# Mixture-of-experts stage of a graph-attention kernel: the router's VectorE order written out, its list built before its experts and biases, and two row groups of the second half loaded and measured early

## Chip, cores and metric

The kernel runs on 1 core of one Trainium2 chip. The metric is the device time of one execution in microseconds (us); the time before is 2988.52 us, the median of 3 runs (2987.83 to 2989.67).

## What is computed

Two layers over x with 4096 rows of 256 columns. Each layer is a dense graph attention over a 4096 x 4096 adjacency matrix, then a feed-forward part; layer 0 has a 30-step recurrence, layer 1 a mixture of six experts of which every row uses two. The change lies wholly in this last part:

```
x = x + _L1_gnn_ref(L1_gnn_t, _layernorm(x, axis=-1), adj, ...)
x = x + _L1_ffn_ref((_layernorm(x, axis=-1))[None], ...)[0]

def _L1_ffn_ref(features, ...):
    rh = relu(features @ router_w1 + router_b1)
    expert_logits = softmax(rh @ router_w2 + router_b2)
    top_w, top_i = top_k(expert_logits, 2)
    routing_weights = softmax(top_w)
    h1 = relu(features x expert_w1 + expert_b1)      # per expert
    h2 = relu(h1 x expert_w2 + expert_b2)
    expert_out = h2 x expert_w3 + expert_b3
    return sum over the two chosen experts of routing_weight * expert_out
```

## The kernel before

**Stages.** Attention of layer 0, the recurrence, two attention passes of layer 1 and the mixture follow each other. Rows are worked in tiles of 128 and in groups of four tiles (512 rows, 512 KB). The mixture splits the eight groups into two halves: groups 0 to 3 (half 0) and 4 to 7 (half 1).

**The router, `route(h, ...)`.** It is a generator: each `yield` marks a step. Its loop over groups `g` measures a group (`over_std`: four `bn_stats` L101, four `bn_aggr` L103, plus an epsilon L105 on VectorE, then a power L106 on GpSimd), one turn later normalises it (`nmr` L1109, four pieces of `n` L1112), stores it to the DRAM tile `nd` (L1115, SyncE's queue), transposes it on TensorE (`tp` L1120), copies it out on ScalarE (`fT` L1121) and writes the row minus one into the sums' tile `acc` (L1122, ScalarE). Another turn later it multiplies by the router's first matrix (`ps_r` L1099), takes the relu (`rh` L1101, ScalarE), multiplies by the second (`ps_l` L1129) and adds the bias on VectorE (`lg` L1132). After the loop comes a chain of small VectorE operations on all rows of the half: softmax, the best two (L1142 to L1162), a running count per expert (L1164 to L1176, four matmuls in between), each row's place in a list sorted by expert (L1179 to L1213). Two one-hot matrices per choice (`ohh` L1219 and L1222, `ohl` L1224) and 32 matmuls (L1229) turn places into the list: for every tile of 128 places the rows to fetch (`source` L1257) and where results go (`dest` L1258). `seen`, `ex` and `expert` (L1238 to L1246) give each tile's expert, `ohe`, `sel` and `bsel` (L1261 to L1271) its biases, `ws` (L1274 to L1279) the routing weights.

**The experts.** There are 37 tiles per half, 74 in all. For tile i, `gather` (L1313) fetches 128 rows of `nd` by `source` with an indirect DMA of GpSimd; `turn` transposes them (`pt` L1324) and copies them on VectorE (`xT` L1326); `fetch` reads the tile's expert into registers (L1333) and copies that expert's first two matrices (`w` L1344, VectorE and ScalarE); `hidden` makes the two hidden layers (`ph` L1352, relu L1363 on ScalarE and L1365 on VectorE); `result` the output (`po` L1373, `ye` L1375) and scatters it (L1376, GpSimd). `combine` adds the weighted results to `acc` (L1402) and writes the output. Half 1's `route` is stepped once per expert tile, so it runs beside half 0's experts.

**What sets the order.** Instructions are put on the engines' queues in an order that a planner works out before the run: among those that it holds ready, the one that stands first in the program. Each engine and SyncE's DMA queue then keep to that order. Inside `tc.manual_schedule(engines=...)` the named engines' instructions keep the program's order among themselves; instructions from outside such a block can still be put between them. In the mixture before only four small matmuls stand in such a block. The attention's end (`u`, `e`, L473 to L627) is outside one as well.

**Data.** Attention loads groups 0 to 3 of `x3d` ahead into the four places of `ring`. Half 1's groups are loaded by `load` through `load_ahead` (L93) into the same places. The tiles of the pool `m_one` take the SBUF that attention's tiles had, in the order in which they are asked for. The experts' 18 weight loads (L1297, 256 KB each) and `b3` (L1298) are written in the program after the first four steps of `route(0)`.

Of the kernel before, what the change touches and what calls it, by code (L numbers as in the profile page):

```python
# [11 lines left out]
F32 = mybir.dt.float32  # L12
# [6 lines left out]
OP = mybir.AluOpType  # L19
# [4 lines left out]
P = 128  # L24
# [22 lines left out]
def gnn_ffn_kernel(ctx: ExitStack, tc: tile.TileContext, a: dict, out: bass.AP):  # L47
# [48 lines left out]
    def over_std(pool, src):  # L96

        st = pool.tile([P, G, 6], F32, name="ln_st")
        mv = pool.tile([P, G, 2], F32, name="ln_mv")
        for r in range(G):  # L100
            nc.vector.bn_stats(st[:, r, :], src[:, r, :])  # L101
        for r in range(G):
            nc.vector.bn_aggr(mv[:, r, :], st[:, r, :])  # L103
        rstd = pool.tile([P, G], F32, name="ln_rstd")
        nc.vector.tensor_scalar(rstd, mv[:, :, 1], EPS, None, op0=OP.add)  # L105
        nc.gpsimd.tensor_tensor(rstd, rstd, mhalf, OP.pow)  # L106
        return rstd, mv
# [877 lines left out]
    def runs_of(t, g):  # L985

        return t[g * GR : (g + 1) * GR, :].rearrange("(p r) c -> p r c", r=G)
# [31 lines left out]
    with ExitStack() as scope:  # L1019
# [1 line left out]
        T = 2 * NH // P + E - 1  # L1021
        one = scope.enter_context(tc.tile_pool(name="m_one", bufs=1))
        bT = one.tile([P, NB], F32, name="bT")
        acc = one.tile([P, NT, C], F32, name="acc")
        ws = one.tile([P, 2, NT], F32, name="ws")
        bsel = [one.tile([P, T, 2 * KC], F32, name=f"bsel{h}") for h in range(2)]
        expert = [one.tile([P, T], I32, name=f"expert{h}") for h in range(2)]
        dest = [one.tile([P, T], I32, name=f"dest{h}") for h in range(2)]
        source = [one.tile([P, T], I32, name=f"source{h}") for h in range(2)]
        ew = [one.tile([P, E, KC, C], F32, name=f"ew{i}") for i in range(3)]  # L1030
        b3 = one.tile([P, E, C], F32, name="b3")
        nd = [dram.tile([NH, C], F32, name=f"nd{h}") for h in range(2)]
        yd = [dram.tile([2 * NH + T * P, C], F32, name=f"yd{h}") for h in range(2)]
# [41 lines left out]
        def over(t, n=NTH, m=E):  # L1075
            return t[:, :, None].to_broadcast([P, n, m])

        def route(h, turned, bank):

            lg = rone.tile([P, NTH, E], F32, name="lg")  # L1080
            rows, stds, fTs, rhs = {}, {}, {}, {}

            def load(g):
                if h * NGH + g not in ahead:
                    load_ahead(x3d, h * NGH + g, runs_of)
                rows[g] = ahead.pop(h * NGH + g)

            load(0)
            load(1)
            for g in range(NGH + 2):  # L1090
                if g + 2 < NGH:
                    load(g + 2)
                if g < NGH:
                    stds[g] = over_std(rwork, rows[g])
                if 2 <= g:
                    ps = bank("ps_r")
# [6 lines left out]
                if 1 <= g <= NGH:  # L1103
                    u = g - 1
                    at = (h * NGH + u) * G
                    t = rows.pop(u)
                    rstd, mv = stds.pop(u)
                    nmr = rwork.tile([P, G], F32, name="nmr")
                    nc.vector.scalar_tensor_tensor(nmr, mv[:, :, 0], -1.0, rstd, op0=OP.mult, op1=OP.mult)  # L1109
                    n = rwork.tile([P, G, C], F32, name="n")  # L1110
                    for r in range(G):
                        nc.vector.tensor_scalar(  # L1112
                            n[:, r, :], t[:, r, :], rstd[:, r : r + 1], nmr[:, r : r + 1], op0=OP.mult, op1=OP.add
                        )
# [102 lines left out]
            for i in range(2):  # L1217
# [20 lines left out]
            nc.vector.tensor_tensor(  # L1238
                seen,
                along[:, :T, None].to_broadcast([P, T, E - 1]),  # L1240
                first[:, None, 1:].to_broadcast([P, T, E - 1]),
                OP.is_ge,
            )
# [13 lines left out]
            nc.vector.tensor_scalar(source[h], sf, float(NH - 1), None, op0=OP.min)  # L1257
            nc.vector.tensor_copy(dest[h], df)  # L1258
            yield
            ohe = rone.tile([P, T, E], F32, name="ohe")  # L1260
            nc.vector.tensor_tensor(  # L1261
                ohe, over(ex, T), along[:, None, :E].to_broadcast([P, T, E]), OP.is_equal
# [18 lines left out]
        with tc.tile_pool(name="r_ps", bufs=1, space=PSUM) as psum, tc.tile_pool(  # L1281
# [187 lines left out]
```

## Time and profile before

| what | value |
|---|---|
| median of 3 runs | 2988.52 us |
| the profiled execution's own time | 2978.01 us |
| its span, first to last instruction | 2976.1 us |
| mean granted TensorE clock | 0.979 |
| PE / DVE / ACT / POOL busy share of the span | 94% / 92% / 83% / 39% |
| last matmul of attention ends | about 2652.6 us from the span's start |
| first expert matmul starts | 2710.47 us |

PE is TensorE's matmuls and PEld its weight loads, DVE VectorE, ACT ScalarE, POOL GpSimd, SP SyncE with its DMA queue; L101 is line 101 of the kernel. The profiled execution is a different one from the timed runs and 10.5 us below their median. Times inside the profile count from the start of its span. A line of a timeline gives the start, the duration (of a run of like instructions, from the first start to the last end), engine, line, operation, what is written and read, and in brackets how long the engine was idle before and what ended it. A line of a table by stage gives for each engine the busy us and the number of instructions, then the granted TensorE clock, the DMA share and GB/s.

### The profile page before, as it was taken

The page shows a single profiled execution, that of the slowest core. Times are in us where ns is not written, and L with a number is a line of the kernel's source. Part 1 is how long each engine was busy: PE and PEld are TensorE (multiplying, and loading weights), DVE is VectorE, ACT ScalarE, POOL GpSimd, SP SyncE. Part 2 cuts the span into 40 slices and gives each one's busy share as a digit, 9 for nine tenths or more (in the row PEclk, how much of TensorE's full clock was granted, in tenths as well). Part 3 has the DMA queues.
Part 4 walks back from the last instruction along what each step waited for, and adds up shares of the span by engine and source line. Part 5 has one row for each costly group of instructions (what it writes and reads, how often), then busy time and mean ns, then how long its engine had stood idle before and what let it go on. Part 6 is the DMA issues. An engine that isn't in the chain of part 4 may idle for free. (4 is left out here: it accounts for less than half of the span.)

```text
span 2976.1 us, 82659 instructions
## 1 busy us (share of the span) xinstructions
PE 2800.0 (94%) x33923; PEld 2562.3 (86%) x33923; DVE 2740.5 (92%) x5769; ACT 2465.1 (83%) x3125; POOL 1157.6 (39%) x1084
## 2 busy tenths in 40 slices
PE   7899999979999999999998999999889999986996
PEld 5899999968888888888887999999789999975995
DVE  7999999999999999999998899999889999986775
ACT  6799999988888888888877999999789999963342
POOL 3000000079999999999982000000200000014663
PEclk9999999989999999999999999999999999997998
DMA  9998885053333333333353031121302132124253
GB/s 292 272 255 243 227 239 154 24 128 68 68 68 68 68 69 68 68 67 70 68 111 119 22 102 57 64 80 34 108 23 91 55 104 88 44 78 147 81 173 135
DMA packets 484451, 320.07 MB, mean 108 GB/s; under 512 B 416590, under 2 KB 445419, under 8 KB 477931
## 3 DMA queue, kind: packets, MB, share of 16 engines
q1 hardware_dynamic: 474034, 290.27, 36.3%
q0 software_dynamic: 7104, 19.41, 2.1%
q8 instruction: 268, 4.39, 0.6%
q10 hardware_dynamic: 2936, 5.11, 0.5%
q14 instruction: 109, 0.88, 0.1%
HBM read 183.00 MB, written 52.04 MB: 79 GB/s over the span
## 5 line engine op out<-in xcount | busy, mean ns | idle before, releaser
L520 PE MATMUL acc<-vals,st 128*128 128x130 f16 x12288 | 1433.2, 218 | 38.3 <-DVE u L473 29.9
L520 PE MATMUL acc<-vals,below 128*128 128x130 f16 x12288 | 1432.9, 221 | 12.8 <-DVE below L574 12.0
L462 ACT ACTIVATE st<-f1b,nf 128x1024 int8<-128x1024 f32 x1265 | 1334.8, 1143 | 33.4 <-PE acc L520 24.1
L520 PEld LDWEIGHTS <-below 128*128 128x128 fp8e4 x12288 | 1176.5, 96 | 52.9 <-issue 46.5
L520 PEld LDWEIGHTS <-st 128*128 128x128 fp8e4 x12288 | 1208.2, 98 | 9.4 <-DVE st L568 7.5
L936 PE MATMUL po<-wT,zT 128*128 128x256 f32 x1920 | 576.1, 382 | 5.8 <-DVE y L876 3.2
L939 PE MATMUL po<-w,zT 128*128 128x256 f16 x3840 | 578.0, 273 | 0.7 <-DMA zT<-z 0.7
L907 POOL TENSOR_TENSOR th<-th,y 128x1024 f32<-128x1024 f32 x232 | 549.1, 2367 | 14.9 <-DVE z_st L916 0.4
L939 PEld LDWEIGHTS <-zT 128*128 128x128 f16 x3840 | 376.7, 98 | 162.0 <-DMA zT<-z 1.4
L574 DVE TENSOR_TENSOR below<-m,st 128x1024 int32<-128x1024 int32 x384 | 470.0, 1224 | 32.6 <-DVE st L568 0.9
L568 DVE TENSOR_TENSOR st<-st,m 128x1024 int32<-128x1024 int32 x384 | 467.3, 1217 | 0.2
L876 DVE SCALAR_TENSOR_TENSOR y<-po,z_rs,bias 128x256 f32<-128x256 f32 x928 | 384.4, 477 | 1.8 <-PE tp L868 0.7
L916 DVE BATCH_NORM_STATS2 z_st<-z 128x6 f32<-128x256 f32 x960 | 335.8, 413 | 0.0
L936 PEld LDWEIGHTS po<-wT,zT 128*128 128x128 f32 x1920 | 291.1, 192 | 15.3 <-ACT zT L923 3.6
L892 ACT ACTIVATE z<-th 128x1024 f32<-128x1024 f32 x240 | 251.7, 1049 | 17.5 <-POOL th L907 16.7
L927 POOL TENSOR_TENSOR z_rs<-z_rs,mhalf 128x4 f32<-128x4 f32 x240 | 244.6, 1019 | 3.1 <-ACT z_rs L926 3.1
L906 ACT ACTIVATE th<-y 128x1024 f32<-128x1024 f32 x232 | 241.7, 1042 | 0.0
L923 ACT COPY zT<-tp 128x512 f32<-128x512 f32 x240 | 140.4, 585 | 90.8 <-PE tp L868 89.7
L460 DVE TENSOR_SCALAR st<-f1b,nf 128x1024 int8<-128x1024 f32 x271 | 201.2, 743 | 7.6 <-PE acc L520 7.6
L759 POOL TENSOR_TENSOR x_rs<-x_rs,mhalf 128x4 f32<-128x4 f32 x8 | 9.4, 1174 | 503.6 <-ACT x_rs L758 503.6
L1044 POOL IOTA along_i<- 128x512 int32 (+1 forms) x5 | 2.8, 556 | 486.7 <-PE acc L520 486.6
L437 POOL MEMSET hs<- 128x4 f32 x3 | 0.3, 99 | 492.8 <-DVE u L490 492.8
(263 smaller groups left out, 3158.8 us busy)
## 6 DMA issues: line engine op xcount, KB each, us to landing
ring<-in_adj_dram SPq DMA_DIRECT2D x64, 1024.0 KB
m<-edges SPq DMA_DIRECT2D x32, 1024.0 KB
f1b<-fd SPq DMA_DIRECT2D x48, 512.0 KB
edges<-m SPq DMA_DIRECT2D x16, 1024.0 KB
y<-yd SPq DMA_DIRECT2D x16, 512.0 KB
ew<-in_L_ffn_expert_w_dram SPq DMA_DIRECT2D x18, 256.0 KB
t<-in_x_dram SPq DMA_DIRECT2D x8, 512.0 KB
old<-in_x_dram SPq DMA_DIRECT2D x16, 256.0 KB
```

Of the source, the lines that this page charges most:

```text
L462: nc.scalar.activation(out, f1, AF.Sign, bias=f2, scale=-1.0)
L520: nc.tensor.matmul(acc[:, i, cols], masked[part][:, at_i // TR, s, rows], v[:, cols], start=(j == 0 and part == 0), stop=(j == NT - 1 and ...
L568: nc.vector.tensor_tensor(above, above, whole, OP.bitwise_and)
L574: nc.vector.tensor_tensor(below, whole, above, OP.bitwise_xor)
L876: nc.vector.scalar_tensor_tensor(t[:, r, :] if end else y[:, g * G + r, :], po[:, r, :], rstd[:, r : r + 1], t[:, r, :] if end else bias, ...
L892: ins = nc.scalar.activation(z, th.pop(u), AF.Silu, scale=0.01)
L906: nc.scalar.activation(th[at], was, AF.Tanh, scale=0.01)
L907: ins = (nc.gpsimd if at else nc.vector).tensor_tensor(th[at], th[at], was, OP.add)
L916: nc.vector.bn_stats(st[:, r, :], z[:, r, :])
L927: nc.gpsimd.tensor_tensor(rs[u], rs[u], mhalf, OP.pow)
L936: nc.tensor.matmul(po[:, r, :], src[:, r * P : (r + 1) * P], wT, start=True, stop=False)
L939: nc.tensor.matmul(po[:, r, :], src16[:, part * G + r, :], w16[:, other, :], start=False, stop=(part == 1 and other == 1),)
```

## The change

- **Memory.** In `m_one`, `acc` and `ws` are now asked for behind the three `ew` tiles, and the `ew` tiles are asked for in reverse.
- **Two loads moved up.** Groups 4 and 5 are loaded into their own rows of `acc` before `route(0)` begins. Groups 6 and 7 are loaded into theirs by `route(1)`; `ring` isn't used for half 1 any more. L1122 writes half 1's `acc` in place.
- **Two measurements moved up.** `measure_other` runs `over_std` for groups 4 and 5 in the last two turns of `route(0)`'s loop; `route(1)` uses the results.
- **Order.** `seen`, `ex` and `expert` move from ahead of `lst` to behind `dest`, for both halves.
- **VectorE's order in `route(0)`.** All its steps are traced in `manual_schedule` blocks for VectorE. The experts, `fetch` and `route(1)` are not.

```diff
-        acc = one.tile([P, NT, C], F32, name="acc")
-        ws = one.tile([P, 2, NT], F32, name="ws")
...
-        ew = [one.tile([P, E, KC, C], F32, name=f"ew{i}") for i in range(3)]
+        ew = [one.tile([P, E, KC, C], F32, name=f"ew{i}") for i in (2, 1, 0)][::-1]
+        acc = one.tile([P, NT, C], F32, name="acc")
+        ws = one.tile([P, 2, NT], F32, name="ws")
...
+            early = {}
+        def rest(g):
+            return acc[:, (NGH + g) * G : (NGH + g + 1) * G, :]
+        def measure_other(g):
+            early[g] = over_std(rone, rest(g), f"_{g}")
...
             def load(g):
-                if h * NGH + g not in ahead:
-                    load_ahead(x3d, h * NGH + g, runs_of)
-                rows[g] = ahead.pop(h * NGH + g)
+                if h:
+                    rows[g] = rest(g)
+                    if g in early:
+                        stds[g] = early.pop(g)
+                    else:
+                        nc.sync.dma_start(rows[g], runs_of(x3d, NGH + g))
+                else:
+                    rows[g] = ahead.pop(g)
...
-                if g < NGH:
+                if g < NGH and g not in stds:
                     stds[g] = over_std(rwork, rows[g])
...
+                if not h and g >= NGH:
+                    measure_other(g - NGH)
                 if 2 <= g:
                     u = g - 2
...
-            seen = rone.tile([P, T, E - 1], F32, name="seen")
-            nc.vector.tensor_tensor(
...
-                OP.is_ge,
-            )
-            ex = rone.tile([P, T], F32, name="ex")
-            nc.vector.tensor_reduce(ex, seen, axis=AX.X, op=OP.add)
-            nc.vector.tensor_copy(expert[h], ex)
             lst = rone.tile([P, T, 2], F32, name="lst")
...
             nc.vector.tensor_copy(dest[h], df)
             yield
+            seen = rone.tile([P, T, E - 1], F32, name="seen")
+            nc.vector.tensor_tensor(
...
+                OP.is_ge,
+            )
+            ex = rone.tile([P, T], F32, name="ex")
+            nc.vector.tensor_reduce(ex, seen, axis=AX.X, op=OP.add)
+            nc.vector.tensor_copy(expert[h], ex)
             ohe = rone.tile([P, T, E], F32, name="ohe")
...
+            for g in range(2):
+                nc.sync.dma_start(rest(g), runs_of(x3d, NGH + g))
             steps = route(0, turned, bank)
-            for _ in range(4):
-                next(steps)
+            with tc.manual_schedule(engines={mybir.EngineType.DVE}):
+                for _ in range(4):
+                    next(steps)
...
-            for _ in steps:
-                pass
+            with tc.manual_schedule(engines={mybir.EngineType.DVE}):
+                for _ in steps:
+                    pass
```

`over_std` gets a name mark so that the two early results have tiles of their own.

More of the change, by code (lines that the diff above doesn't have):

```diff
@@ L94, in load_ahead, with over_std @@
         ahead[g] = t
-    def over_std(pool, src):
+    def over_std(pool, src, mark=""):
         st = pool.tile([P, G, 6], F32, name="ln_st")
-        mv = pool.tile([P, G, 2], F32, name="ln_mv")
+        mv = pool.tile([P, G, 2], F32, name=f"ln_mv{mark}")
         for r in range(G):
@@ L103, in over_std @@
             nc.vector.bn_aggr(mv[:, r, :], st[:, r, :])
-        rstd = pool.tile([P, G], F32, name="ln_rstd")
+        rstd = pool.tile([P, G], F32, name=f"ln_rstd{mark}")
         nc.vector.tensor_scalar(rstd, mv[:, :, 1], EPS, None, op0=OP.add)
@@ L1236, in route @@
                 yield
-            seen = rone.tile([P, T, E - 1], F32, name="seen")
[L1238 to L1241, printed above, removed]
-                OP.is_ge,
-            )
-            ex = rone.tile([P, T], F32, name="ex")
-            nc.vector.tensor_reduce(ex, seen, axis=AX.X, op=OP.add)
-            nc.vector.tensor_copy(expert[h], ex)
             lst = rone.tile([P, T, 2], F32, name="lst")
@@ L1259, in route @@
             yield
+            seen = rone.tile([P, T, E - 1], F32, name="seen")
+            nc.vector.tensor_tensor(
+                seen,
+                along[:, :T, None].to_broadcast([P, T, E - 1]),
+                first[:, None, 1:].to_broadcast([P, T, E - 1]),
+                OP.is_ge,
[3 more added lines that the diff above has]
+            nc.vector.tensor_copy(expert[h], ex)
             ohe = rone.tile([P, T, E], F32, name="ohe")
```

## The prediction, made before the change was run

> **What bounds the kernel now.** The page's slices show all engines busy until the last tenth, so I read that end by stage: granted clock and busy time.
>
> ```profile
> 2640.00:2660.00 20.00, 12.84 (x220) 12.56 (x217) 14.99 (x31) 4.00 (x6) 7.05 (x20) 0.93 0.11 27
> 2660.00:2680.00 20.00, 16.38 (x72) 10.07 (x72) 10.99 (x48) 10.35 (x16) 7.15 (x13) 0.82 0.81 257
> 2680.00:2700.00 20.00, 2.71 (x28) 2.54 (x29) 16.50 (x53) 6.96 (x10) 0.00 (x0) 0.61 0.63 243
> 2700.00:2720.00 20.00, 13.26 (x78) 11.19 (x78) 14.29 (x64) 4.36 (x10) 13.83 (x14) 0.62 0.34 112
> 2720.00:2740.00 20.00, 20.00 (x150) 18.40 (x149) 12.19 (x41) 9.19 (x21) 11.43 (x12) 1.00 0.38 126
> ```
>
> The first count is PE's, the third DVE's. From 2720 PE is always busy; the 58 us before are the front, where each step waits for one other. From 2682 to 2704 that is DVE: PE has 2.71 of 20 us. Next, DVE's timeline there.
>
> ```profile
> 2684.03 0.26 DVE L1158 TENSOR_TENSOR hot<-lg,top 128x96 f32<-128x96 f32 x1
> 2684.33 0.26 DVE L1159 TENSOR_TENSOR hot<-hot,order 128x96 f32<-128x96 f32 x1
> ...
> 2685.78 0.26 DVE L1158 TENSOR_TENSOR hot<-lg,top 128x96 f32<-128x96 f32 x1
> 2685.95 0.17 DVE L1274 TENSOR_TENSOR ws<-top,top 128x16 f32<-128x16 f32 x1
> 2686.07 0.26 DVE L1159 TENSOR_TENSOR hot<-hot,order 128x96 f32<-128x96 f32 x1
> ...
> 2690.10 0.35 DVE L1238 TENSOR_TENSOR seen<-along,first 128x185 f32<-128x185 f32 x1
> ...
> 2691.89 1.07 DVE L1265 TENSOR_TENSOR sel<-ohe,bT 128x888 f32<-128x888 f32 x1
> ...
> 2693.36 1.07 DVE L1271 TENSOR_REDUCE bsel<-sel 128x148 f32<-128x888 f32 x1
> ...
> 2703.25 0.17 DVE L1257 TENSOR_SCALAR source<-sf 128x37 int32<-128x37 f32 x1
> ```
>
> The list ends with `source` at 2703.42. Instructions that the list doesn't need stand between its own. GpSimd's and PE's timelines show what follows.
>
> ```profile
> 2703.05 1.01 POOL L106 TENSOR_TENSOR ln_rstd<-ln_rstd,mhalf 128x4 f32<-128x4 f32 x1 [33.17 <-DVE sf L1256]
> 2704.31 1.61 POOL L1313 DMA_INDIRECT gx<-nd,source  x1 [0.25 <-DVE ln_mv L103]
> ```
>
> ```profile
> 2665.13 3.08 PE L1099 MATMUL ps_r<-fT,g_w 128*128 128x512 f32 x4
> ...
> 2670.70 1.88 PE L1099 MATMUL ps_r<-fT,g_w 128*128 128x512 f32 x4
> ...
> 2710.47 1.91 PE L1352 MATMUL ph<-xT,w 128*128 128x128 f32 x8
> ...
> 2716.28 1.88 PE L1099 MATMUL ps<-fT,g_w 128*128 128x512 f32 x4
> ```
>
> The first gather waits for a power that half 1 asked for. After 2710.47 half 1's router stands on PE between expert tiles. From there a microsecond at the first expert matmul is one at the end, as PE has no gap until 2764 and each tile then costs 2.87 us of PE.
>
> **The change, part by part** (negative is a gain).
>
> *Router loop in program order.* Before, DVE made `n` of group 2 (ended 2669.84) ahead of `lg` of group 0 (2670.52). In program order `lg`(0) comes first, and behind it wait the measurement of group 3 (four at 0.34, four at 0.09, the epsilon: 1.8 us), then `n`(2) (1.3), `lg`(1), `n`(3). PE and ScalarE wait for these. `n`(2) ends near 2673.6. Transposes and copy-out add 1.2 us, so `ps_r`(2) starts near 2674.9 where it started at 2674.28. From there PE's cycle of 3.65 us (between `lg` at 2674.46, 2678.11 and 2681.77) goes on, only shifted. Value +0.6. Ends: -0.3 (the group-2 statistic ahead of the first `n`, 0.33, is gone) and +1.5 (both late groups pay). The two added measurements (2 x 1.8 us) lie in DVE's waits of 3.47 us for `lg`(2) and `lg`(3): 0; uncovered they cost 3.6.
>
> *The list without strangers.* Between `shift` (2690.02) and the first `ohh` (2694.86) DVE takes 4.84 us. The list's own steps at their start-to-start times (0.20, 0.29, 0.55, 0.38, 0.20, 0.20, 0.20, 0.10) sum to 2.1: 2.7 gained. Behind the last list matmul, `lst` (2701.52) to `source`'s end takes 1.90, without half 1's statistics 1.4: 0.5. Together -3.2. But what isn't in the block may still be put between, and two groups measured early are ready: `n` of groups 4 and 5, eight pieces of 0.33 us start to start. The first needs a buffer whose store was issued at 2679.66 and landed within 6.6 us (the longest of the eight `nd` stores), so by 2686.3; the planner will hold it ready somewhere in the list's second half.
> What does a stranger cost? The Trainium skill, "VectorE: DVE Perf Modes", section "The DRAIN you can't avoid", has the next operation wait until the pipe is empty after every operation; then a piece costs its whole 0.33. The rows above differ: two dependent steps lie 0.30 apart alone (2684.03 to 2684.33) and 0.29 apart with a 0.17 us `ws` between (2685.78 to 2686.07), which came free. About 0.12 fits into a gap, so a piece costs 0.21. I count five inside the list, the other three in the wait for the last matmuls: +1.0 (by the page +1.65, which would make the sum below -5.6). Ends: none, or eight pieces and eight statistics of groups 6 and 7 (16 x 0.21 = 3.4), or one piece so early that in-order DVE stands until 2686.3, 3.9 us after `lg`(3). Value -2.2, from -3.2 to +0.7.
>
> *The first gather.* The power of group 4 ran from 2703.05 to 2704.06; without it the gather starts 0.25 after `source`: -0.6. Ends -0.6 and 0 (a power of group 6 takes its place).
>
> *Experts and biases later.* Behind `source` DVE has `seen`, `ex`, `expert` (0.8 us), `ohe`, `sel`, `bsel` (2.5), then the weights' round trip to ScalarE. `expert` to the end of DVE's first `w` copy took 3.4 us (2691.42 to 2694.85), so both are done about 4.2 us behind `source`. The first expert matmul stood 7.05 us behind it, 6.4 without the power. Cover 2.2: 0; without cover up to 1.
>
> *Half 1's router ahead of the experts.* Before, `n` of group 4 came at 2704.75, and only 3 of 32 transposes stood ahead of 2710.47. Behind it a group takes 0.88 (`tp`) + 1.72 (`ps`) + 0.81 (logits) = 3.4 us of the saturated PE. With `n`(4) and `n`(5) between 2687 and 2701, PE and ScalarE, idle there, can do them. If all of both groups goes ahead, 7.0 us leave the bound stretch (with what ran at half clock); if only the remaining transposes of both, 1.9. I take the transposes of both and one group's `ps` and logits: -4.0. Ends -7 and 0 (`n`(5) behind the list and PE's queue in the old order).
>
> *Data.* Two loads (issue 0.64 us each: 2.57 for four) go on SyncE's queue behind 2652.2, when attention's last matmuls free the SBUF under `acc`; DMA is nearly idle until 2661, the queue's next entry waits for `e` at 2660.98, and the first user comes near 2676: 0. The weight loads start at 2664.45 as before; two loads less in the full stretch to 2692 bring groups 6 and 7 about 2.8 us sooner (1 MB at 370 GB/s). The `ew` tile that now lies over attention's last sums is loaded last, from 2674: 0. Even an uncovered load costs only what measuring it late would. `acc` in place: four ScalarE operations of 1.14 us wait for `n` and leave an idle stretch (2694 to 2698) for one with 9.2 of 20 us busy; relu has 1.1 us of slack: 0, uncovered up to 1 each.
> *Half 1's list* keeps its free order; `bsel`(1) behind `source`: 0, +-1.5 for the 3 us that PE loses near 2780.
>
> Sum: 0.6 - 2.2 - 0.6 - 4.0 = -6.2, so 2978.0 becomes 2971.8 in the profile, and the median of 2988.5 (10.5 above this execution) 2982.3. All low ends give -11, all high ends +2.2.
>
> **Rivals.**
> 1. *Everything runs ahead* (0.20): list -3.2, gather -0.6, router -7: about 2977.5. For it: PE and ScalarE idle from 2684. Against: `n`(5) must stand in the list.
> 2. *The strangers change only their names* (0.30): statistics and pieces of half 1 fill the list's gaps as `sel` did, and PE gains only transposes: 0.6 + 0.2 - 0.6 - 1.9 = -1.7, 2986.8. For it: the planner filled nearly every gap before. This is also the case where the fixed order doesn't do what it says.
> 3. *Slower* (0.12): PE starves in the router loop and loses its clock. `ps_r` takes 3.08 us at 2665 (granted 0.5) and 1.88 at 2670. The Trainium skill, "TensorE: Matmul & The Clock Gate", section "What's actually happening", halves the clock after an idle window of about 3.4 us; the trace agrees (0.50 behind the idle from 2652.6 to 2662.9). At half clock each of three groups pays 1.2 (`ps_r`), 1.1 (transposes), 0.4 (logits), and DVE's serial order 1 per group: about +11; less list and gather, with nothing run ahead, +8.3: 2996.8. It decides once PE waits over 3.4 us for `n`; my longest gap is near 1. By the page's rule the risk is real, by the row (granted 1.00 from 2668 to 2684 with PE busy for 12.4 of the 16 us) the clock holds.
> The forecast has 0.38.
>
> **The numbers.** A measurement of this kernel tells about 0.2% (6 us) from no change. The forecast lies on that line: with rival 1 and most of its own spread, faster 0.48; same 0.40 with rival 2; slower 0.12. Range 2975.5 to 2993.5: all gains and a little more below; above, the high ends and part of rival 3.
>
> **What would show it.** Right: `source` ends 2 us or more sooner; no power ahead of the first gather; `tp` and `ps` of half 1 ahead of the first `ph`; fewer of them after. Wrong: `sel`-sized gaps in the list, or DVE waiting for the `nd` store before `n`(4); `ps_r` at 3 us in the loop; first `ph` early but the end not, which would put the bound elsewhere, near 2780 or in GpSimd's queue at the end.

## The result, and the profile after

| | median, us (runs) | ratio to before | difference, us |
|---|---|---|---|
| first comparison | 2985.57 (22), before 2988.91 (22) | 0.9987 [0.9981, 0.9993] | -3.9 [-5.7, -2.1] |
| the same kernel again (first experiment) | 2971.19 (13), before 2978.19 (58) | 0.9976 [0.9968, 0.9985] | -7.1 [-9.5, -4.5] |

Intervals are of 95%; the differences are those of the ratio and its ends times before's median. The change makes the kernel faster, by 0.13% in the first comparison (within 0.2%) and by 0.24% in the second. The forecast was -6.2.

The profiled execution after took 2989.25 us (span 2987.5), the one before 2978.01. That difference isn't the change's, as a second profile shows (first experiment): the trace after holds single pauses in which every engine stops (below). So I compare stages, with attention's last matmul as the zero; it ends at 2652.60 before, at 2654.65 after. First the table by stage, in the same stretches as before but 2.05 us later.

```profile
2662.05:2682.05 20.00, 16.51 (x72) 10.14 (x72) 14.71 (x67) 10.53 (x16) 7.92 (x15) 0.82 0.83 277
2682.05:2702.05 20.00, 4.98 (x48) 4.00 (x48) 16.67 (x53) 2.13 (x4) 0.89 (x1) 0.61 0.64 238
2702.05:2722.05 20.00, 16.16 (x78) 12.53 (x79) 11.78 (x43) 7.49 (x17) 13.12 (x12) 0.71 0.35 111
```

PE has 2.3 us more work in the list's stretch and 2.9 more in the next: some of half 1's router moved ahead. DVE has 3.7 us more in the router loop, the two early measurements, and the clock is 0.82 there as before. Next DVE's timeline in the list.

```profile
2691.77 0.17 DVE L1212 SCALAR_TENSOR_TENSOR shift<-first,ends 128x6 f32<-128x6 f32 x1
...
2693.99 0.77 DVE L1234 TENSOR_TENSOR ohh<-along,hi 128x592 f32<-128x592 f16 x1
...
2697.31 0.41 DVE L1125 TENSOR_SCALAR n<-acc,ln_rstd,nmr 128x256 f32<-128x256 f32 x1
...
2699.45 1.05 DVE L1125 TENSOR_SCALAR n<-acc,ln_rstd,nmr 128x256 f32<-128x256 f32 x3
...
2700.93 0.23 DVE L1253 COPY lst<-ps_r 128x74 f32<-128x74 f32 x1
2701.08 0.42 DVE L101 BATCH_NORM_STATS2 ln_st<-acc 128x6 f32<-128x256 f32 x1
2701.41 0.18 DVE L1255 SCALAR_TENSOR_TENSOR none<-lst,place 128x37 f32<-128x37 f32 x1
...
2702.86 0.15 DVE L1262 TENSOR_SCALAR source<-sf 128x37 int32<-128x37 f32 x1
```

`shift` to `ohh` takes 2.22 us where it took 4.84: nothing stands between the list's own steps there. One piece of `n` stands among the one-hots, three lie in the wait for PE, and statistics of group 6 stand between `lst` and `source`. Counted from attention's end, `source` is done 2.46 us sooner. Last GpSimd's and PE's timelines behind it.

```profile
2703.90 1.24 POOL L1332 DMA_INDIRECT gx<-nd,source  x1 [20.96 <-DVE n L1125]
2705.44 1.85 POOL L1332 DMA_INDIRECT gx<-nd,source  x1 [0.30 <-issue]
```

```profile
2703.21 3.62 PE L1112 MATMUL ps<-fT,g_w 128*128 128x512 f32 x4
2707.00 0.41 PE L1343 MATMUL pt<-ident,gx 128*128 128x128 f32 x2 [0.17 <-DMA gx<-nd,source]
2709.18 0.44 PE L1343 MATMUL pt<-ident,gx 128*128 128x128 f32 x2 [1.77 <-DMA gx<-nd,source]
...
2709.68 1.31 PE L1371 MATMUL ph<-xT,w 128*128 128x128 f32 x8
```

No power stands ahead of the first gather, yet it starts 0.89 us behind `source`, as before; the second takes 1.85 us instead of 0.95. Group 4's first layer runs ahead of the experts. PE waits for gathered rows, as before, ahead of the first `ph` (0.17 and 1.77 us here, 1.55 and 1.24 before), and once more behind it, where it had no gap before. The first `ph` stands 2.84 us sooner. Behind tile 6 pauses like this one cost over 15 us against a second profile of the same kernel; the table by stage shows one.

```profile
2813.00:2814.00 1.00, 1.00 (x6) 0.62 (x5) 0.00 (x0) 0.00 (x0) 0.86 (x1) 1.00 0.46 131
2814.00:2815.00 1.00, 0.08 (x1) 0.00 (x0) 0.20 (x1) 0.18 (x1) 0.00 (x0) 1.00 0.32 131
```

In the second row PE, ScalarE, VectorE and GpSimd all stand nearly still, at a granted clock of 1.00 and with DMA moving.

### The profile page after: what moved, and what is told of

It reads as the page before. It is cut to its first block, busy times and chain, and to the rows that moved or that the text cites. A ratio compares the mean times of both kernels' runs of the same rounds, so it can differ in the third digit from the quotient of the medians.

```text
span 2987.5 us, 82648 instructions
## 1 busy us (share of the span) xinstructions
PE 2805.7 (94%) x33923; PEld 2560.7 (86%) x33923; DVE 2738.2 (92%) x5769; ACT 2462.9 (82%) x3125; POOL 1157.9 (39%) x1084
```

## The experiments

All numbers of this table are counted from attention's end. Row one is before's own time; the others are us against it (minus is sooner). Tile 6, 27 and 40 are the starts of their scatters on GpSimd (counted from 0), the span's end is the end less attention's end. Timed is the ratio's difference from 1 times before's median, as above. The last three runs are full of pauses, so their traces are not in it.

| kernel | `source` | first `ph` | tile 6 | tile 27 | tile 40 | span's end | timed |
|---|---|---|---|---|---|---|---|
| before | 50.82 | 57.87 | 93.36 | 164.69 | 204.17 | 323.50 | |
| changed, first profile | -2.46 | -2.84 | -2.09 | +0.03 | +2.40 | +9.35 | -3.9 |
| changed, again | -2.47 | -2.90 | -3.85 | -5.85 | -6.84 | -7.72 | -7.1 |
| order only | -2.12 | -2.95 | -1.88 | -3.90 | -4.76 | -5.80 | -5.1 |
| early only | +0.84 | +0.02 | -3.39 | -3.09 | -3.04 | -4.97 | -4.5 |
| one block | -0.93 | -1.22 | -3.70 | -5.71 | -6.80 | -7.66 | -7.4 |
| experts in the wait, both halves | +1.11 | +0.69 | -0.52 | -0.91 | -0.80 | -1.15 | +0.3 |
| the same, half 0 alone | +1.12 | +0.69 | -0.49 | +1.25 | -1.67 | -2.97 | -2.1 |
| `n` on ScalarE | -2.64 | -2.93 | -7.94 | -9.96 | -10.97 | -12.00 | -10.1 |
| long block, behind | -2.74 | +4.88 | -1.55 | -1.95 | -1.94 | -3.00 | -2.7 |
| long block, in the wait | +2.93 | +2.41 | -4.01 | -4.00 | -4.00 | -4.67 | -4.2 |

The span's end and the timed difference agree within 2 us in all but the first profile, so the columns can be read as parts of the time.

From the first `ph` to tile 6 the lead has three parts, and they have to be kept apart: PE's work, its idle time, and what it loses at half clock. In these traces the granted clock is 1.00 or 0.50 from attention's end on. I weigh PE's busy time by it (us, worked out from each trace):

| first `ph` to tile 6 | length | PE's work at full clock | PE idle | lost at half clock |
|---|---|---|---|---|
| before | 35.49 | 33.14 | 0.00 | 2.35 |
| changed, first profile | 36.24 | 31.28 | 1.99 | 2.97 |
| changed, again | 34.54 | 31.14 | 1.69 | 1.71 |
| order only | 36.56 | 34.20 | 0.19 | 2.17 |
| early only | 32.08 | 31.08 | 0.00 | 1.00 |
| one block | 33.01 | 31.22 | 0.30 | 1.49 |
| `n` on ScalarE | 30.48 | 29.84 | 0.65 | 0.00 |
| `n` on ScalarE, again | 32.86 | 30.16 | 0.28 | 2.41 |

Two executions of one kernel, with a front equal to 0.05 us, differ in the last column by 1.26 and 2.41 us. So that column isn't all the edit's, and one trace of each kernel can't tell how much of it is. The first 5 us behind the first `ph` of the last two rows, in this order:

```profile
2708.44:2713.44 5.00, 4.35 (x35) 3.91 (x36) 4.23 (x20) 2.12 (x7) 4.18 (x5) 1.00 0.29 82
2705.34:2710.34 5.00, 5.00 (x24) 4.99 (x25) 2.76 (x10) 1.25 (x4) 4.17 (x5) 0.52 0.28 82
```

**The changed kernel again.** No edit.

> The changed kernel once more, for a second profile. In its first profile the front is 2.46 us earlier at `source`'s end, 2.84 at the first expert matmul and 2.09 at tile 8 (all counted from attention's last matmul), but at tile 73 it is 10 us later, through single pauses of 0.3 to 1.9 us of all engines at once behind tile 26. Theory A (the pauses belong to the one execution, not to the change): the front's three numbers come back within 0.3 us, the pauses are elsewhere or fewer, and the time is 2 to 5 us below the kernel before. Theory B (the change disturbs the expert tiles): the pauses stand at the same tiles again (27, 31, 39) and the time is no better than before.

Theory A. The front repeats (`source` -2.47, first `ph` -2.90), tile 6 stands at -3.85, and behind it the lead only grows. Against this trace, the first profile lost 17.3 us by the last scatter (10.49 and -6.82): 1.76 ahead of tile 6, 1.26 of them at half clock, and the rest to pauses behind it.

**Order only.**

```diff
-            for g in range(2):
-                nc.sync.dma_start(rest(g), runs_of(x3d, NGH + g))
...
-                if not h and g >= NGH:
-                    measure_other(g - NGH)
```

> Only the order: VectorE's fixed order, experts and biases behind the list, the new order in memory; no group of half 1 is loaded or measured early. Theory A (the list is what gains: the strangers cost 2.2 us there, and running half 1's router ahead of the experts is worth nothing): `source` ends 2 to 2.7 us sooner than before, the first expert matmul 2 to 3 us sooner, the time 2 to 4 us below the kernel before, as the whole change has it. Theory B (the two groups measured early give a good part, as the prediction's term of -4.0 said): the list gains but the time is at most 1 us below before, 3 above the whole change. As `n` of groups 4 and 5 can't be in the list now, this also shows what the list takes with no piece of `n` inside: 19.5 us from `lg`(3) to `source` with four of them, 18.8 to 19.3 without if each cost 0.05 to 0.2.

-5.1 us [-7.4, -3.0]: more than theory A expected and no clear loss against the whole change. `lst` stands at 46.29 without any `n` in the list and at 46.27 with four pieces. That doesn't make the pieces free: here statistics of group 4 stand in the same places, one among the one-hots and the others in the wait for PE. From first `ph` to tile 6 it loses 1.07 us where the whole change gains 0.95, so the early groups are worth 2.0 us there: 3.06 of PE's work and 0.46 of clock, less 1.50 of idle time.

**Early only.**

```diff
-            with tc.manual_schedule(engines={mybir.EngineType.DVE}):
-                for _ in range(4):
-                    next(steps)
+            for _ in range(4):
+                next(steps)
...
+            seen = ...    # to expert[h], ahead of lst again
             lst = rone.tile([P, T, 2], F32, name="lst")
```

> The other part alone: two groups of half 1 loaded and measured early in the place of the sums; VectorE's order is the planner's, and experts and biases stand ahead of the list as before. Theory A (only the list's strangers count): the list from `lg`(3) to `source` takes 21 to 22.5 us as before (21.65), and the time is within 1.5 us of the kernel before, or up to 2 slower if pieces of `n` come into the list besides. Theory B (early measurement gains by itself): 3 us or more faster than before, with PE's first expert matmul no earlier but less of half 1's router after it.

Theory B, -4.5 us [-6.3, -2.4]: my theory that only the list counts falls. `source` is 0.84 *later* and the first `ph` where it was, yet tile 6 stands 3.39 sooner, 2.06 of it by less PE work and 1.35 by less time at half clock. PE's timeline:

```profile
2699.47 1.07 PE L1133 MATMUL tp<-ident,n 128*128 128x128 f32 x4
2701.27 1.12 PE L1133 MATMUL tp<-ident,n 128*128 128x128 f32 x4 [0.73 <-ACT fT L1134]
2702.18 3.62 PE L1112 MATMUL ps<-fT,g_w 128*128 128x512 f32 x4
2705.59 0.63 PE L1133 MATMUL tp<-ident,n 128*128 128x128 f32 x2
...
2708.66 1.94 PE L1369 MATMUL ph<-xT,w 128*128 128x128 f32 x8
```

Group 4's transposes and first layer lie ahead of the first `ph`, where PE waited before. Of the edit's own effect, what counts is how much of half 1's router is left behind it; whether the busier PE also brought the full clock back sooner isn't shown.

**One block.**

```diff
             with tc.manual_schedule(engines={mybir.EngineType.DVE}):
                 for _ in range(4):
                     next(steps)
-            for i in range(3):
...
+                for i in range(3):
...
-            with tc.manual_schedule(engines={mybir.EngineType.DVE}):
                 for _ in steps:
                     pass
```

> The whole change with one fixed block where it has two: the first four steps of the router loop and the rest under one order, so that group 3's statistics and group 2's normalisation can no longer be put ahead of group 0's logits. By the prediction's step (+0.6 for the router loop; the changed kernel has -0.3 there) `lg`(3) ends 0.9 us later than in the changed kernel, and all behind it with it: `source` 0.9 later, the time about 1 us above the changed kernel, 2 to 3 below before. Rival: VectorE's waits for the transposes and for PE hide it, and `lg`(3) and the time are as in the changed kernel, within 0.2 us at `lg`(3).

`lg`(3) ends 1.53 us later than in the changed kernel (30.59 and 29.06), more than expected, and `source` too; the time is the changed kernel's all the same (-7.4 [-9.5, -5.4]). DVE's timeline shows the order that the prediction had assumed:

```profile
2670.85 0.18 DVE L1147 TENSOR_TENSOR lg<-ps_l,g_w 128x24 f32<-128x24 f32 x1 [3.52 <-PE ps_l L1144]
2670.95 1.40 DVE L101 BATCH_NORM_STATS2 ln_st<-ring 128x6 f32<-128x256 f32 x4
```

Group 3's statistics wait here behind `lg`(0). In the changed kernel a second block isn't tied to the first, so its `n`(2) stands ahead of `lg`(0). The 1.68 us at the first `ph` are 0.15 at tile 6: PE idles 1.39 us less between them.

**Experts and biases in the wait for the list's last matmuls, both halves.** `seen` to `bsel` stand ahead of `lst` in VectorE's fixed order.

```diff
+            seen = ...    # to bsel[h]
             lst = rone.tile([P, T, 2], F32, name="lst")
```

> The whole change with one part undone in both halves: the tile's expert and biases (`seen` to `bsel`) stand ahead of `lst` again, in VectorE's fixed order right behind the last `ohl`, where it waits for PE's last list matmuls; so in half 0 `sel` and `bsel` no longer run beside the second gather. In the changed kernel `source` to first gather takes 0.88 us, the first gather 1.24 and the second 1.85, where a later one takes 0.95; `sel` (1.08) and `bsel` (1.07) run beside the second. Theory A (VectorE's long operations slow GpSimd's descriptor work): the second gather takes 0.95, the rows of tiles 2 and 3 come 0.9 earlier, PE's wait of 1.60 us at tile 3 shrinks, and tile 8 starts 0.5 to 1.3 us sooner than in the changed kernel. Theory B (the second gather is slow by itself): 1.85 again and tile 8 as before. For half 1's list, theory A' (putting these steps behind the list also took PE's wait of 1.25 us for `ohh`, worth 2.0 us between tiles 16 and 24): the 2.0 us are lost again, so that the time as a whole is 1 to 2 us above the changed kernel; rival: they stay, since they come from the two early groups.

**The same in half 0 alone.** In half 1 they stay behind.

> As the run before with expert and biases in VectorE's wait for the last list matmuls, but in half 0 alone; half 1 keeps them behind the list. Theory A: the front gains as there (second gather 0.95 us, tile 8 0.5 to 1.3 sooner than in the changed kernel) and the 2.0 us at half 1's list stay, so the time is 0.5 to 1.3 us below the changed kernel. Theory B (order in half 1 isn't what took PE's wait there): tile 16 to 24 loses as in the other run. If the planner now puts pieces of `n` between `lst` and `source`, `source` ends up to 0.4 later and eats part of it.

Theory A's gather came, its gain didn't: +0.3 [-2.4, 2.7] and -2.1 [-4.8, 0.3]. GpSimd's and DVE's timelines of the second of the two:

```profile
2706.09 1.24 POOL L1338 DMA_INDIRECT gx<-nd,source  x1 [24.50 <-DVE ln_st L101]
2707.64 0.95 POOL L1338 DMA_INDIRECT gx<-nd,source  x1 [0.30 <-issue]
```

```profile
2700.41 1.08 DVE L1268 TENSOR_TENSOR sel<-ohe,bT 128x888 f32<-128x888 f32 x1 [0.68 <-PE tp L1133]
2701.41 0.42 DVE L1369 COPY w<-ew 128x512 f32 x1
2701.75 1.07 DVE L1274 TENSOR_REDUCE bsel<-sel 128x148 f32<-128x888 f32 x1
2702.73 0.23 DVE L1279 COPY lst<-ps_r 128x74 f32<-128x74 f32 x1
```

The second gather is back at 0.95. But the wait is too short for what came into it: two pieces of `n`, a wait of 0.68 and a copy of weights besides the six steps. `lst` stands at 49.46 behind attention's end instead of 46.27, and five long strangers follow it, so `lst` to `source`'s end takes 2.48 us instead of 2.08 and the list loses 3.6 us. For half 1 the pair tells two things apart, having one front (tile 6 at -0.52 and -0.49). PE waits 1.23 and 1.24 us for `ohh`, so the order there doesn't by itself remove that wait. At tile 40 they stand at -0.80 and -1.67: in this pair the gain near tile 40 comes with the order. (The +1.25 of half 0 alone at tile 27 is PE work done sooner: 1.98 us more of it lie between tiles 6 and 27, and 1.93 less between 27 and 40.)

**`n` of groups 4 and 5 on ScalarE.** The rest is the whole change.

```diff
                     for r in range(G):
+                        if h and u < 2:
+                            nc.scalar.activation(
+                                n[:, r, :], t[:, r, :], AF.Identity, bias=nmr[:, r : r + 1], scale=rstd[:, r : r + 1]
+                            )
+                            continue
                         nc.vector.tensor_scalar(
```

> The whole change, and `n` of groups 4 and 5 is made by ScalarE (idle from 2684 to 2697) in place of VectorE: eight pieces leave VectorE, and both groups' transposes and the first router layer can run on PE ahead of the first expert tile. Theory A (the prediction's step: a microsecond of half 1's router that runs ahead is one at the end): 3 to 4 us less PE work behind the first expert matmul than in the changed kernel, so tile 8 is 3 us sooner and the time 3 us below the changed kernel. Theory B (the first tiles wait for gathers, which GpSimd issues one each 1.25 us after `source`, so work that leaves PE there becomes waiting): tile 8 sooner by at most 1.5 us, with PE waiting for DMA at tiles 1 to 3. The first gather begins 0.88 us behind `source` in both, though no `n` is on VectorE then, if that gap is GpSimd's own.

Theory A: 0.9966 [0.9954, 0.9978], -10.1 us, on six runs; tile 6 stands 4.1 us ahead of the changed kernel's with the same first `ph`. Of these, 1.30 are PE's work, 1.04 its idle time and 1.71 the clock, which stood at 1.00 in this execution and not in the repeat below. PE's timeline:

```profile
2699.38 1.07 PE L1138 MATMUL tp<-ident,n 128*128 128x128 f32 x4
2700.25 3.13 PE L1112 MATMUL ps<-fT,g_w 128*128 128x512 f32 x4
2703.21 0.60 PE L1138 MATMUL tp<-ident,n 128*128 128x128 f32 x4
2704.16 1.06 PE L1149 MATMUL ps<-g_w,rh 128*128 128x6 f32 x8 [0.34 <-ACT rh L1114]
...
2708.44 1.13 PE L1376 MATMUL ph<-xT,w 128*128 128x128 f32 x8 [0.56 <-DVE xT L1350]
```

All of group 4 and group 5's transposes lie ahead of the first `ph`: PE's gaps between the gathers are filled with work that the tiles then don't have to carry. ScalarE begins `n`(4) at 2689.93, behind a wait of 6.48 us for the store of an earlier `n`. The first gather begins 0.88 behind `source` with no `n` near it.

**The long block, experts behind the list.** `n` on ScalarE with `nmr` made beside the measurement, and the second fixed block held open over the first three expert tiles.

```diff
-            with tc.manual_schedule(engines={mybir.EngineType.DVE}):
-                for _ in steps:
-                    pass
+            fixed = tc.manual_schedule(engines={mybir.EngineType.DVE})
+            fixed.__enter__()
+            for _ in steps:
+                pass
...
+            if i == 2:
+                fixed.__exit__(None, None, None)
```

> A candidate: `n` of groups 4 and 5 on ScalarE with their scale made beside the measurement, and the fixed block reaching on over the first three expert tiles, so that no statistic of groups 6 and 7 can stand in the list; expert and biases behind the list. Compared with the kernel that only moves `n` to ScalarE (10 us below the kernel before; tail from attention's end 311.5 us): theory A (a stranger between `lst` and `source` costs 0.1 us each, and more of the router ahead of the first expert tile is a gain of the same size): `source` 0.5 to 0.7 us sooner, both groups' transposes and first layers ahead of the first expert matmul, tile 4 sooner by 1 to 2.5 us, the time 1 to 3 us lower. Theory B (PE's order puts so much of it at half clock ahead of the first expert tile that this waits for it): the first expert matmul 1 to 3 us later and nothing gained in sum. `sel` still runs beside the second gather, which then takes 1.5 to 1.85 us.

**The long block, experts in the wait.** The same, with half 0's `seen` to `bsel` ahead of `lst`.

> The same candidate, with half 0's expert and biases in VectorE's wait for the last list matmuls. In the two runs that put them there alone, copies of expert weights came in too and `lst` stood behind them: 49.45 us behind attention's end instead of 46.28. The longer fixed block keeps those copies behind `source`. Theory A: `lst` at 46.1 to 46.6, `source` as in the other candidate or up to 0.3 later, second gather 0.95 us as nothing long runs beside it, tiles 2 and 3 sooner by up to 0.9; the time 0 to 1 us below the other candidate. Theory B: logits of group 4 stand ahead of `sf` in VectorE's order here and wait for PE, so `source` is 1 to 3 us later and the time 1 to 3 us above the other candidate.

Theory B in both: -2.7 us [-4.8, -0.6] and -4.2 [-6.0, -2.1], 6 to 7 us short of the kernel with `n` on ScalarE alone in its first comparison, 2 to 4 in its second. With experts behind, the list has no stranger: `lst` to `source`'s end took 1.48 us (2.08 in the changed kernel).

```profile
2699.90 0.23 DVE L1263 COPY lst<-ps_r 128x74 f32<-128x74 f32 x1 [1.39 <-PE ps_r L1254]
...
2701.20 0.18 DVE L1272 TENSOR_SCALAR source<-sf 128x37 int32<-128x37 f32 x1
```

Then DVE waits, first in the one with experts behind, then in the other:

```profile
2709.98 0.18 DVE L1157 TENSOR_TENSOR lg<-ps,g_w 128x24 f32<-128x24 f32 x1 [5.05 <-PE ps L1154]
...
2712.61 0.43 DVE L1374 COPY w<-ew 128x512 f32 x1 [1.45 <-PE ps L1114]
```

```profile
2703.21 0.20 DVE L1294 SCALAR_TENSOR_TENSOR df<-df,none 128x37 f32<-128x37 f32 x1
2707.10 0.18 DVE L1157 TENSOR_TENSOR lg<-ps,g_w 128x24 f32<-128x24 f32 x1 [3.69 <-PE ps L1154]
2707.20 0.17 DVE L1296 TENSOR_SCALAR sf<-df 128x37 f32<-128x37 f32 x1
```

The logits of group 4 come from a later step of `route(1)`, outside the block, so the planner could put them anywhere, and put them ahead of the weights' copies in one and inside the list in the other. There in-order DVE waits 5.05 and 3.69 us for PE. Inside the list, one stranger that waits costs 3.7 us, the changed kernel's seven that don't 0.6.

**Experts ahead in half 1 alone**, half 0 as changed; **`n` on ScalarE again**; and the first of these once more.

> The whole change with expert and biases put ahead of the list again in half 1 alone; half 0, with its fixed block, is as in the changed kernel. Theory A (moving them behind half 1's list is what gains 2.0 us between tiles 16 and 27, and the 1.0 us near tile 40 too, as all kernels with the 1.0 us have them behind): the front is the changed kernel's within 0.1 us up to tile 10 (3.8 us ahead of the kernel before), then the lead stays at 3.8 or less to the end, and the time is 3 us above the changed kernel. Theory B (the order of half 1's experts doesn't matter; the planner packs half 1's list otherwise because of what comes before it): the lead grows to 5.8 or 6.8 us all the same.

> The candidate with `n` of groups 4 and 5 on ScalarE and nothing else, once more, beside the run above: its time stood on few runs (0.9966, interval 0.9954 to 0.9978). If the trace's account of it is right (7.9 us ahead of the kernel before at tile 4, 11 at tile 73, 12 at the end), it is 10 to 12 us below the kernel before again, and its front repeats to 0.1 us. If those few runs were lucky, it is near the changed kernel's 7.

> Experts and biases ahead of the list in half 1 alone, once more: the trace of the first look is full of single pauses of all engines of up to 1.9 us and can't be read between tiles 10 and 27. In a trace without them: theory A (their place in half 1 gains the 2.0 us between tiles 16 and 27 and the 1.0 us near tile 40): the lead over the kernel before is 3.8 us at tile 10 and still 3.0 to 4.0 at tile 73, PE waits 0.8 to 1.3 us for `ohh` in half 1's list, and the time is 3 us above the changed kernel's (4 below before where that was 7 below). Theory B: no wait for `ohh`, lead 5.8 us at tile 27 and 6.8 at 73.

Timed -4.5 [-7.2, -1.8], -6.6 [-9.3, -3.9] and -3.6 [-6.3, -0.6]. All three traces are full of pauses, and before's median stood at 2992.27 and 2995.28 there, where it was 2978 in the other experiments. The repeat of `n` on ScalarE was below the 10 to 12 us expected; its front repeats (`source` at 48.23, first `ph` at 54.96; 48.18 and 54.94 in its first run), but tile 6 stands at 87.82 instead of 85.42. No pause lies there: the 2.40 are the 2.41 of the clock in the table above. So the first trace of `n` on ScalarE flatters it by that much against its repeat.

For half 1's experts the question stays half open. PE waits for `ohh` in both runs with them ahead (0.79 and 1.07 us), as in the two other kernels that have them ahead (early only, in the wait in both halves). With them behind, the wait is gone in the changed kernel, order only, one block and `n` on ScalarE; but it is there, with 1.24 or 1.25 us, in the three kernels whose front differs more (in the wait in half 0 alone, the two long blocks). The granted clock goes with the wait. First PE's timeline and the table by stage before, then PE's timeline in the changed kernel again:

```profile
2779.94 1.26 PE L1229 MATMUL ps<-ohh,ohl 128*128 128x74 f16 x16 [1.25 <-DVE ohh L1222]
2780.02:2783.43 3.41, 3.41 (x25) 3.23 (x25) 2.33 (x11) 0.00 (x0) 0.98 (x1) 0.50 0.15 53
```

```profile
2773.53 1.28 PE L1244 MATMUL ps<-ohh,ohl 128*128 128x74 f16 x16
```

Within 2 us behind the wait the clock stands at 0.50 for 3.41 us, in all six traces of the table with a wait of 1.23 to 1.25, before among them, and PE loses 1.71 us of work by it. In those without the wait it stays at 1.00 from tile 6 to tile 27. That the two come together is what the traces show; in this table no trace has one without the other. The gain near tile 40 is one wait of PE too, for DVE's relu `h`:

```profile
2853.46 1.16 PE L1352 MATMUL ph<-h,w 128*128 128x128 f32 x8 [1.38 <-DVE h L1365]
```

In the changed kernel again it is 0.39. It behaves likewise: the gain is in neither kernel of the table with the experts ahead in half 1, and in all with them behind but the long blocks. So their place behind the list was needed in every kernel here and was not enough. I take it that the planner's packing of the half decides; no run isolates it.

## Why the prediction was right and where it was wrong

The sum was near: -6.2 forecast, -3.9 and -7.1 measured, -7.7 by the trace without pauses. Of its four terms only the list's came out as forecast. The account of that trace, from the table: -2.90 at the first `ph`, -0.95 to tile 6, -2.00 to tile 27, -0.99 to tile 40, -0.88 from there to the end.

- **Router loop, +0.6.** Measured -0.29 at `lg`(3). I had read the fixed order as one; it is two blocks that aren't tied to each other. In one block it is +1.24. The early measurements were free, as said: they lie in DVE's waits for `lg`(2) and `lg`(3), of which 0.19 and 0.40 us are left.
- **The list, -2.2.** From `lg`(3) to `source` 21.65 us became 19.48: -2.17. Its parts came out too. Without a stranger (long block, experts behind) the list takes 18.69, 2.96 less than before, where I had 3.2. The changed kernel's strangers cost the other 0.79, where I had 1.0: 0.60 between `lst` and `source`, 0.19 among the one-hots; those in the wait for PE are free. I had them as pieces of `n`; most were statistics. The price was right for long ones, 0.41 to 0.43 us each: five of them, with no other, stretch `lst` to `source`'s end from 1.48 to 2.48 us in both kernels with experts in the wait, 0.20 each, where I had 0.21. The changed kernel's three long ones make up its 0.60, so its four short ones of 0.15 to 0.17 us cost next to nothing. The Trainium skill's "VectorE: DVE Perf Modes" (section "The DRAIN you can't avoid"), read as a wait behind every operation, gave 0.33; the section adds that an operation that isn't held starts earlier, and these rows agree. A stranger costs what it doesn't find of the gap between two dependent steps.
- **First gather, -0.6.** Measured 0. `source` to first gather is 0.88 to 0.90 us in every kernel whose trace was read, with a power that ends 0.25 ahead of it (before), with one that ends 0.99 ahead (order only: 2699.49 + 1.01, gather 2701.49) and without. The power lay inside that time. I had taken the instruction that ended last for the one that was waited for. `source` to the first `ph` still shrank, from 7.05 to 6.62 us; the first gather itself, 1.61 us before and 1.24 in the changed kernel, is as large as 0.37 of that 0.43, though no run isolates it.
- **Experts and biases later, 0.** They did delay something that I hadn't listed: `sel` beside the second gather makes it 1.85 us instead of 0.95, and PE waits for rows behind the first `ph` (1.60 us in the second trace).
- **Half 1's router ahead, -4.0.** Measured -0.95 behind the first `ph`: 2.00 us less PE work, 1.69 more idle time, 0.64 less lost at half clock. So the mechanism is right and the size was twice too large: ten of the 32 transposes and group 4's first layer went ahead (before, four transposes did, not three), but not its logits and the rest of group 5, since `n`(5) stood behind `source`. What I left out is that PE would then wait for gathers behind the first `ph`. Early groups alone move 2.06 us of work and with `n` off DVE it is 3.30; the other parts of their -3.39 and -5.01 by tile 6 are mainly the clock, 1.35 and 2.35.
- **"A microsecond at the first expert matmul is one at the end."** This step failed, and the sum rests on it. One block: 1.68 later there, 0.15 at tile 6. Early only: 0.02 and -3.39. Long block: 4.88 later and -1.55. Ahead of tile 6 PE's idle time, the work put into it and the granted clock decide; from there the lead carries up to half 1's list.
- **Data, 0.** The two loads went out at 2666.23, behind `nd`(0) on SyncE's queue, not at 2652, and groups 6 and 7 came no sooner. Neither was waited for. `acc` in place cost nothing that shows.
- **Half 1's list, 0 +-1.5.** Measured -2.00 between tiles 6 and 27, and -0.99 more near tile 40, in a stretch that I held untouched: more than my own +-1.5, which the sum of the ends left out. The "3 us that PE loses" were there: 1.25 of waiting for `ohh`, as DVE ran the six one-hots in a row, and 1.71 at half clock behind it. After, relu and copies stand between. From tile 6 to 27 PE idles 1.13 us less and loses no clock (-1.71), and does 0.84 more work: -2.00. Near tile 40 the wait for `h` shrinks from 1.38 to 0.39. Why the waits fall is open, as told above. The last 0.88 lie in the final loads of `yd`, with no edit near; from the last scatter to the end takes 24.6 to 26.4 us in the traces of the table.

Of the rivals, the second (only names change) falls by the list, the third by the clock in the router loop: 1.00 in each 4 us from 2670 to 2686, with `ps_r` at 1.88 to 1.96 us. But I had the clock at risk only behind a wait of over 3.4 us. It stood at 0.50 behind a wait of 1.25 between tiles 10 and 16, and the forecast had no term for losing or gaining that. The first is what `n` on ScalarE comes near to: -10.1 and -6.6 timed, where I gave that rival -11, and 3.30 us of work moved, where I gave -7.

So the forecast was right in part by luck: the gather's 0.6, the router loop's 0.9 and the router's 3.05 were off one way or the other, and half 1's list with what follows (-3.87) made up for them.

The best version here is the change with `n` of groups 4 and 5 on ScalarE, whatever the clock did in its first trace: -10.1 [-13.7, -6.6] and -6.6 [-9.3, -3.9] us in two comparisons.

## What to carry to other kernels

When a saturated engine follows an idle stretch, ask which of its later work can go into the stretch; when its first instruction starts tells little. Fix the order of a chain of small dependent steps only as far as it reaches: a stranger of 0.4 us that is ready cost 0.2 here, a short one next to nothing, one that waits costs the whole wait, and a second block isn't tied to the first. The instruction that ended just ahead of another isn't what it waited for until a run without it shows so. Before a stage's gain in one trace is put down to an edit, weigh that stage by its granted clock, and take a second trace.

## What the runs showed of the hardware

- **Two-input operations of VectorE slow GpSimd's gathers.** The second gather takes 0.95 us with no `sel` beside it, 1.22 with 0.4 us of it, 1.85 with all of `sel` (1.08) and a copy of weights (0.42). With `bsel`, a reduce of 1.08 us, beside it (long block, experts behind) it takes 0.95. That kernel also has a gather beside five one-hots in a row, from 2774.57 to 2778.97, all of two inputs and with no copy among them; it takes 5.05:

```profile
2774.77 5.05 POOL L1343 DMA_INDIRECT gx<-nd,source  x1 [0.31 <-PE ph L1382]
```

  The Trainium skill, "SBUF — State Buffer", section "Who interferes with whom", says that a VectorE operation with two SBUF inputs contends with a GpSimd instruction that reads SBUF, and infers that descriptor work is left alone by it. Here it isn't: the gather, which reads its row numbers from SBUF, takes five times as long.
- **The granted clock falls behind short waits of PE, and not in every execution.** It stands at 0.50 for 3.41 us behind PE's waits of 1.23 to 1.25 us for `ohh` in six traces, a loss of 1.71 us each; behind before's wait of 1.38 us for `h` near tile 40 it stays at 1.00. Around the first expert tiles it differs between two executions of one kernel, by 1.26 and 2.41 us of PE's time.
- **Pauses of all engines**, 0.3 to 1.9 us each on PE, at a granted clock of 1.00. They come in some comparisons and not in others: over 15 us by them in the changed kernel's first profile, none in its second. Before's median is 2978 us where the traces have none and 2989 to 2995 where they have many. A chip of the same number gave 2978.19 and 2992.27, so it doesn't seem to be the chip alone. What they are stays open, and whether they take back part of a gain: the changed kernel gained 7.1 us without and 3.9 with them, and the intervals overlap.
- **The front repeats to 0.05 us** from attention's end to the first gather in two executions of one kernel, while their own times differ by 21 us. Stages counted from a common event show differences that the span hides.
